# A product made three times over the same bank, in the scan of a four-layer hybrid network

## The chip, the core and the metric

The kernel runs on one core of a Trainium2 chip. The metric is the device time of one execution in microseconds (us). The core has five engines that run side by side, each with its own queue in program order: TensorE (PE; its weight loads are listed apart as PEld), VectorE (DVE), ScalarE (ACT), GpSimd (POOL) and SyncE (SP). ScalarE, SyncE and GpSimd also issue DMA transfers; in the profile a queue's own steps have a q behind the engine's name (ACTq). A pair of terms that come up often: a unit of the scan is one step of the list described below; a bank is a 128 x 512 float32 piece of PSUM, the memory that TensorE writes its products to.

## The reference

Four images of 96 channels and 64 x 64 pixels pass four layers: a selective scan in four directions, a deformable convolution, a Fourier mixing with a quantized feed-forward, and a linear attention with a second feed-forward. The change lies in the first layer's scan. Cut to it:

```python
delta = jax.nn.softplus(dts + delta_bias[None, :, :, None])
def step(h, inp):
    d_t, u_t, b_t, c_t = inp
    dA = jnp.exp(d_t[..., None] * A)
    h = dA * h + (d_t * u_t)[..., None] * b_t[:, :, None, :]
    y = jnp.einsum('bkdn,bkn->bkd', h, c_t)
    return (h, y)
```

There are 192 channels d, 16 states n per channel, 4 directions k, and 4096 pixels in sequence. Every channel's delta times u is spread over its 16 states and multiplied by b there.

## The kernel before

**The units.** `Layer0.scan` (line 773) runs over 1536 units: 4 images, 4 directions, 4 pieces of 1024 pixels, 3 groups of 64 channels, and in each group 8 units of 8 channels. A unit holds 8 channels x 16 states on the 128 partitions and 1024 pixels along the free dimension. Its steps, by method and line:

- `fetch` (823) issues, four units ahead, all on ScalarE's queue: `bc` (b and c of a piece, once in 24 units), `du` (line 845, two tiles at the first unit of each group, so once in 8 units), and `da` (line 858, delta spread over the states, each unit). `du` has delta u in three bf16 parts whose sum is the float32 value, 3 x 32 rows on 96 partitions, for 32 channels and 1024 pixels.
- `decay` (860, line 863) makes exp(A delta) on ScalarE, in place.
- `inflow` (865, line 869) spreads delta u over the states on TensorE. The stationary table `rep` has a 1 where row p, taken modulo 32, is the channel of the output partition. So one product of 96 rows both adds the three parts and copies each channel to its 16 states. Two products of 512 columns fill the two banks of `db`, of which there are two buffers.
- `recur` (878) multiplies `db` by b in place (line 882) and runs the recurrence along the pixels (line 885), both on VectorE.
- `weigh` (889, lines 892 and 894) keeps the last state and multiplies the states by c, on GpSimd.
- `total` (896, lines 907 and 912) sums over the states on TensorE, for two units at a time. `settle` and `store` copy the sum out and send it to DRAM.

**What sets the order.** In iteration n of the scan the program emits, in this order, the total of the units n-5 and n-4 (when n is odd), the product and the decay of unit n+1, the loads of unit n+4, the recurrence of n, and the weighing of n-2. A product of unit n+1 writes a buffer that the recurrence of unit n-1 has used, so it waits for that; the multiplication of unit n+1 comes after the recurrence of unit n on VectorE.

**The side work.** After every unit, steps of two other streams of work are put in: `ends` (the preparation of the next images, then layers 2 and 3) and `middle` (what follows the scan, and the deformable convolution). Which steps, and how many, is decided at build time by a planner, the class `Clock` (198). It keeps an estimated end of the work queued on each engine. Every step of the scan books its estimate with `clock.add`, every side step books what its `cost(...)` says. A side step may go in only if the estimated end of each engine that it needs is not further ahead of now than `AHEAD` (for TensorE 1.0 us), and now moves on by at least `PACE` = 4.7 us each unit:

```python
def has_room(self, work, ready):
    now = self.now()
    idle = self.idle if self.own is None else self.own
    if self.own is None and work[DVE] and self.beside >= BESIDE:
        return False
    first = next((e for e in (PE, ACT, DVE, POOL) if work[e]), None)
    if ready > (now if first is None else max(self.ends[first], idle)):
        return False
    return all(not w or e <= now + a for w, e, a in zip(work, self.ends, AHEAD))
```

The product of a unit books 0.9 us on TensorE (line 866), and its estimated end is also the earliest start that the planner gives the multiplication of that unit. What is left of the two streams when the units are done runs behind the scan. Steps of the side work on TensorE that are named later: the 3 x 3 convolution of layer 0 (line 653), the weighting of the sampled pixels (1237) and the Fourier matrices (1327).

## Time and profile before

| what | value |
|---|---|
| median of 3 runs | 9941.68 us (9924.21 to 9967.65) |
| the profiled execution | 9884.11 us, its span 9882.0 us |
| granted TensorE clock, mean | 0.761 |
| before the first product of a unit | 327 us |
| from the first product to the last | 8063 us |
| after it | 1492 us |
| the two products of a unit, busy time in all | 1191.5 us in 3072 instructions |
| a `du` load's issue on ScalarE's queue | 0.735 us median, 384 of them |

Times in the profile are from one execution. The busy time of an engine is the time in which it works on an instruction; a TensorE instruction's end is modelled, and a float32 product is recorded as two instructions. "PEclk" or "granted clock" is the share of full speed that TensorE's clock was granted. In a group of instructions the columns are line, engine, operation, output and inputs with their shapes and the count, then busy time in us and mean in ns of one, then the idle time of the engine ahead of it and what ended most of that. The chain is followed back from the last instruction to what released it, step by step.

### The profile page before, as it was taken

How to read it: one execution, taken by the hardware profiler on the slowest of the kernel's cores; microseconds unless marked ns; L12 is line 12 of the kernel's file. 1: busy time of each engine (PE TensorE's matmuls, PEld its weight loads, DVE VectorE, ACT ScalarE, POOL GpSimd, SP SyncE). 2: the span in 40 equal slices, each digit the busy share in tenths (PEclk: the TensorE clock that was granted, in tenths of full speed). 3: DMA queues.
4: the chain of work that ended last, by engine and by line, in shares of the span. 5: the costliest groups of instructions: out<-in, count | busy, mean ns of one | idle time of the engine just before them, and what ended most of it. 6: DMA issues, size and time to landing. Idle time of an engine off the chain costs nothing.

```text
span 9882.0 us, 101184 instructions
## 1 busy us (share of the span) xinstructions
PE 7523.3 (76%) x36536; PEld 3441.1 (35%) x36536; DVE 6913.6 (70%) x4545; ACT 4182.3 (42%) x5734; POOL 6722.5 (68%) x4947
## 2 busy tenths in 40 slices
PE   7565866686756679777678788777888777999797
PEld 2111311121123344211136553213565321687283
DVE  0488688877888887788888888788888887122111
ACT  3563655464544334555432334443323444211424
POOL 0695589657789997688899976567989556176101
PEclk9555856686767789766678898777898877899586
DMA  1566677666777877776787886667877756343010
GB/s 46 141 179 167 164 194 193 171 168 170 188 192 202 206 193 194 186 194 182 190 210 195 216 190 171 156 164 182 216 201 204 172 144 146 94 134 113 13 52 7
DMA packets 775689, 1606.32 MB, mean 163 GB/s; under 512 B 249333, under 2 KB 339561, under 8 KB 773078
## 3 DMA queue, kind: packets, MB, share of 16 engines
q10 hardware_dynamic: 300672, 985.79, 40.1%
q1 hardware_dynamic: 400790, 387.50, 14.6%
q0 software_dynamic: 73728, 226.57, 8.5%
q8 instruction: 290, 4.75, 0.2%
q14 instruction: 209, 1.71, 0.1%
HBM read 1343.23 MB, written 256.29 MB: 162 GB/s over the span
## 4 chain that ended last, share of the span: by engine, by line
PE 35%; POOL 19%; DVE 16%; DMA 15%; issue 8%; ACT 6%; ACTq 1%; SPq 1%; DVEq 0%; POOLq 0%
POOL hh L894 9%; PE ps L1237 8%; DVE hh L885 7%; DMA da<-de 5%; POOL g L1215 4%; PE pc L653 4%; DVE db L882 4%; PE f L1327 3%; DMA du<-du 3%; PE py L912 2%; PE po L1115 2%; PE db L869 2%; DMA g<-table,idx 1%; DVE g L1224 1%; POOL lw L742 1%
## 5 line engine op out<-in xcount | busy, mean ns | idle before, releaser
L894 POOL TENSOR_TENSOR hh<-hh,bc 128x1024 f32<-128x1024 f32 x1536 | 3652.2, 2379 | 331.5 <-DVE hh L885 215.3
L885 DVE TENSOR_TENSOR_SCAN hh<-da,st,db 128x1024 f32<-128x1024 f32 x1152 | 2703.7, 2347 | 345.3 <-ACT da L863 220.0
L882 DVE TENSOR_TENSOR db<-db,bc 128x1024 f32<-128x1024 f32 x1536 | 1868.8, 1217 | 586.6 <-PE db L869 584.0
L863 ACT ACTIVATE da<-da,w_al 128x1024 f32<-128x1024 f32 x1536 | 1740.1, 1146 | 913.0 <-DMA da<-de 530.7
L869 PE MATMUL db<-du,rep 96*128 96x512 bf16 x3072 | 1191.5, 481 | 1181.1 <-DVE hh L885 1072.0
L1215 POOL DMA_INDIRECT g<-table,idx x1152 | 1442.5, 1252 | 490.2 <-issue 223.5
L1237 PE MATMUL ps<-w_ident,g 128*96 128x128 f32 x9216 | 1236.6, 299 | 291.5 <-DVE g L1224 160.1
L912 PE MATMUL py<-hh,w_fold 128*32 128x512 f32 x6144 | 1223.6, 802 | 173.4 <-POOL hh L894 80.0
L1237 PEld LDWEIGHTS ps<-w_ident,g 128*96 128x96 f32 x9216 | 1185.9, 183 | 400.9 <-DVE g L1224 198.1
L869 PEld LDWEIGHTS <-rep 96*128 96x128 bf16 x3072 | 209.2, 103 | 2608.9 <-DVE hh L885 1783.5
L885 DVE TENSOR_TENSOR_SCAN hh<-da,db 128x1024 f32<-128x1024 f32 x384 | 878.1, 2287 | 89.7 <-ACT da L863 48.3
L1244 ACT COPY st<-ps 96x384 f32<-96x384 f32 x384 | 182.5, 476 | 1451.9 <-PE ps L1237 1349.8
L1224 DVE TENSOR_TENSOR g<-g,wt 128x3456 f32<-128x3456 f32 x128 | 526.0, 4109 | 334.2 <-DMA g<-table,idx 306.7
L892 POOL COPY st<-hh 128x1 f32<-128x1 f32 x1152 | 279.4, 243 | 696.1 <-DVE hh L885 667.9
L653 PE MATMUL pc<-pad,wc 96*128 96x512 f32 x1152 | 526.7, 607 | 27.1 <-DMA wc<-wc_d 24.8
L741 POOL TENSOR_TENSOR w<-w,ex 128x512 f32<-128x512 f32 x192 | 264.6, 1378 | 393.6 <-ACT w L738 383.1
L1473 POOL CAST xqf<-fl 96x512 fp8e5<-96x512 f32 x64 | 45.3, 716 | 652.6 <-DVE fl L1431 545.0
L912 PEld LDWEIGHTS py<-hh,w_fold 128*32 128x32 f32 x6144 | 178.7, 125 | 815.9 <-issue 430.0
L765 DVE TENSOR_TENSOR du<-ex,du 128x512 bf16<-128x512 f32 x192 | 275.2, 1433 | 189.7 <-ACT du L763 179.3
L731 PE MATMUL pd<-xd,dtw 7*64 7x512 f32 (+1 forms) x512 | 332.4, 955 | 49.9 <-DVE rl L744 39.9
L744 DVE SCALAR_TENSOR_TENSOR rl<-pd,lw 128x512 f32<-128x512 f32 x192 | 130.0, 677 | 291.3 <-POOL lw L742 288.7
L761 POOL TENSOR_TENSOR ex<-ex,du 128x512 f32<-128x512 f32 x192 | 233.0, 1213 | 136.2 <-ACT du L759 135.7
(239 smaller groups left out, 9345.4 us busy)
## 6 DMA issues: line engine op xcount, KB each, us to landing
da<-de ACTq DMA_DIRECT2D x1536, 512.0 KB
du<-du ACTq DMA_DIRECT2D x384, 192.0 KB
bc<-bcd ACTq DMA_DIRECT2D x128, 512.0 KB
du<-du SPq DMA_DIRECT2D x128, 384.0 KB
y<-yb SPq DMA_DIRECT2D x384, 128.0 KB
de<-rl SPq DMA_DIRECT2D x128, 256.0 KB
m<-in_dft SPq DMA_DIRECT2D x128, 256.0 KB
du<-du SPq DMA_DIRECT2D x128, 192.0 KB
```

The source lines that it names most:

```text
L653: nc.tensor.matmul(pp, lhsT=wc[:, q, g * 128 : (g + 1) * 128], rhs=pad[:, r0 + dy : r0 + dy + NR, dx : dx + W], start=(q == 0), stop=(q == 8),
L731: nc.tensor.matmul(o, lhsT=dtw[rows, q, m], rhs=xdbl[q, j][rows], start=True, stop=True)
L863: self.net.nc.scalar.activation(u.da, u.da, AF.Exp, scale=self.al[:, a : a + 1])
L869: self.net.nc.tensor.matmul(db[:, h, :], lhsT=self.rep[:96, u.s % 4, :], rhs=u.du[u.s // 4][:, h * CH : (h + 1) * CH], start=True, stop=True,)
L882: nc.vector.tensor_mul(u.db, u.db, u.bc[:, 0, :])
L885: nc.vector.tensor_tensor_scan(u.along(u.hh), u.along(u.da), u.along(u.db), first, ALU.mult, ALU.add)
L894: self.net.nc.gpsimd.tensor_mul(u.hh, u.hh, u.bc[:, 1, :])
L912: nc.tensor.matmul(py[p0 : p0 + 32], lhsT=self.fold[:, u.i, :], rhs=hc[:, h * CH : (h + 1) * CH], start=u.sums["add"] is None and u.i == 0 ...
L1215: nc.gpsimd.indirect_dma_start(out=g[:, k, :], out_offset=None, in_=self.tables[b % 2], in_offset=bass.IndirectOffsetOnAxis(ap=idx[:, 9 * ...
L1224: nc.vector.tensor_mul(g4, g4, w4.unsqueeze(2).to_broadcast([128, 36, C]))
L1237: nc.tensor.matmul(pt[:, k, :], lhsT=g[:, k0 + k, c * C : (c + 1) * C], rhs=net.ident, start=(c == 0), stop=(c == 3),)
L1327: nc.tensor.matmul(pt[64 * part : 64 * part + 64, c, :], lhsT=d[:, :, c0 + c], rhs=matrix[:, 64 * part : 64 * part + 64], start=True, stop ...
```

## The change

The products of a unit are made three times over, one set behind the other into the same two banks, each of them starting the bank anew, so that the last set stands. They have 128 rows instead of 96. The rows 96 to 127 of the table are set to zero, and the rows 96 to 127 of each `du` tile are filled by a second load of 32 rows of the first part, on the same queue, so that finite numbers meet the zeros. The planner's entry for the product goes from 0.9 to 1.8 us.

```diff
     rep = (p[:, None, None] % 32 == 8 * np.arange(4)[None, :, None] + p[None, None] % 8).astype(f)
+    rep[96:] = 0.0
...
-                t = sp.tile([96, T], BF16, name=f"du{u.key}_{q}", tag=f"du{q}")
-                nc.scalar.dma_start(t, self.du_d[b][k][:, c0 + 32 * q : c0 + 32 * q + 32, ts])
+                t = sp.tile([128, T], BF16, name=f"du{u.key}_{q}", tag=f"du{q}")
+                src = self.du_d[b][k][:, c0 + 32 * q : c0 + 32 * q + 32, ts]
+                nc.scalar.dma_start(t[:96], src)
+
+                nc.scalar.dma_start(t[96:], src[0])
...
-        u.spread = self.net.clock.add(PE, 0.9, self.scanned[1])
+        u.spread = self.net.clock.add(PE, 1.8, self.scanned[1])
         db = self.ps.tile([128, 2, CH], F32, name=f"db{u.key}", tag="db", bufs=2)
-        for h in range(2):
+
+        for h in 3 * (0, 1):
             self.net.nc.tensor.matmul(
                 db[:, h, :],
-                lhsT=self.rep[:96, u.s % 4, :],
+                lhsT=self.rep[:, u.s % 4, :],
```

## The prediction

> **What bounds the kernel now.** I read the busy shares first, then the stages, the chain of work that ended last, the groups and the waits around the db product, and last the timeline of TensorE.

> ```profile
> PE 7523.3 (76%) x36536; PEld 3441.1 (35%) x36536; DVE 6913.6 (70%) x4545; ACT 4182.3 (42%) x5734; POOL 6722.5 (68%) x4947
> ...
> PEclk9555856686767789766678898777898877899586
> ```

> No engine is full over the span, so the shares name no bound. What stands out is PEclk: TensorE is granted full speed only part of the time. The windows by stage (columns: stretch, length, busy time of PE, PEld, DVE, ACT and POOL with counts, granted clock, DMA share, GB/s), cut at the first and the last db product:

> ```profile
> 327.00:8390.00 8063.00, 6000.84 (x27253) 2459.51 (x27252) 6562.89 (x4169) 3618.22 (x4759) 6226.98 (x4535) 0.75 0.73 184
> 8390.00:9882.00 1492.00, 1294.92 (x8868) 903.77 (x8866) 319.70 (x325) 418.29 (x799) 458.54 (x377) 0.81 0.24 68
> ```

> The scan takes 8063 us for 1536 units, 5.25 us each; VectorE is busy 81% of it, GpSimd 77%, TensorE 74%, at a mean clock of 0.75. The 1492 us after it hold no product of the changed kind; TensorE alone is busy there. The chain:

> ```profile
> PE 35%; POOL 19%; DVE 16%; DMA 15%; issue 8%; ACT 6%; ACTq 1%; SPq 1%; DVEq 0%; POOLq 0%
> POOL hh L894 9%; PE ps L1237 8%; DVE hh L885 7%; DMA da<-de 5%; POOL g L1215 4%; PE pc L653 4%; DVE db L882 4%; PE f L1327 3%; DMA du<-du 3%; PE py L912 2%; PE po L1115 2%; PE db L869 2%; DMA g<-table,idx 1%; DVE g L1224 1%; POOL lw L742 1%
> ```

> The chain changes engines all the time, and the product itself (L869) is only 2% of it. Its group, its reader and the two waits between them:

> ```profile
> L885 DVE TENSOR_TENSOR_SCAN hh<-da,st,db 128x1024 f32<-128x1024 f32 x1152 | 2703.7, 2347 | 345.3 <-ACT da L863 220.0
> L882 DVE TENSOR_TENSOR db<-db,bc 128x1024 f32<-128x1024 f32 x1536 | 1868.8, 1217 | 586.6 <-PE db L869 584.0
> ```

> ```profile
> PE db L869 <- DVE hh L885: 1072.0, 492, 15.3
> PE db L869 <- DMA du<-du: 92.2, 25, 23.0
> DVE db L882 <- PE db L869: 584.0, 256, 21.4
> ```

> (Columns of the last: us in total, times, longest.) Both directions occur. In 492 units TensorE stands idle until a scan sets a db buffer free, 2.2 us each on average. In 256 units VectorE stands idle until the product is there, 2.3 us each. In between lie about 790 units in which neither shows an idle wait.

> [...] two stretches side by side, first windows, then TensorE's timeline (start, duration, ..., idle time before it):

> ```profile
> 2855.00:2866.00 11.00, 8.60 (x60) 4.71 (x58) 7.04 (x5) 8.91 (x12) 10.28 (x6) 1.00 0.63 162
> 2867.00:2894.00 27.00, 14.38 (x49) 5.65 (x50) 25.29 (x14) 6.23 (x6) 25.47 (x15) 0.50 0.91 222
> ```

> ```profile
> 2864.20 0.61 PE L869 MATMUL db<-du,rep 96*128 96x512 bf16 x2 [2.20 <-DVE hh L885]
> ...
> 2867.77 1.04 PE L869 MATMUL db<-du,rep 96*128 96x512 bf16 x2 [1.97 <-DVE hh L885]
> ```

> At clock 1.00 the pair takes 0.61 us, at 0.50 it takes 1.04 us. [...] 0.61 us less one isolated product (the shortest on record is 0.38 us) leaves 0.23; 1.04 less one at half clock (at most 0.63) leaves 0.41. [...] I take 128 rows instead of 96 at no time.

> **The change, part by part.**

> **Four more products per unit.** At full clock a unit's product goes from 0.61 to 0.61 + 4 x 0.216 = 1.47 us, at half clock from 1.04 to 1.04 + 4 x 0.427 = 2.75 us. Over 1536 units that is 1327 us of TensorE time at full clock. Most lies beside other work: from the moment a buffer comes free, VectorE is busy for a whole unit, 1.22 + 2.35 = 3.57 us, before it needs the result. A product that starts on time ends 2.1 us early instead of 2.96 at full clock, still 0.8 early at half. The 492 units with an idle TensorE (2.2 us) cover it too. Cover is gone where TensorE comes late. On the chain, L869 has 2% of 9882 = 198 us; that grows by the ratio 0.86/0.61 = 1.41 at full and 1.71/1.04 = 1.64 at half clock, so by 279 to 325: I take **+285**. Check from the waits: 256 late units x 0.86 = 220. Of the other 790 units some become late; I take 60 of them at 0.86, **+50**. Bounds of the two together: 0 (all of it moves into idle time) and 1536 x 0.86 = 1321.

> **The clock.** [...] Between 2867 and 2894 us TensorE is busy 14.4 of 27 us with six pairs; four more products each at half clock add 6 x 1.71 = 10 us, which makes 24.6 of 27[...]. I estimate the scan's mean clock at 0.90 after, instead of 0.75. TensorE has 35% of the chain, 3459 us, of which at most 1295 lie after the scan, so 2164 in it. If those scaled with the clock, a factor 0.75/0.90 would save a sixth, 360 us. But the lines that carry the chain on TensorE (L1237, L653) sit in stretches that already run fast:

> ```profile
> 1200.00:1600.00 400.00, 255.74 (x670) 43.55 (x670) 340.10 (x220) 233.35 (x322) 355.33 (x257) 0.58 0.75 192
> 3600.00:4000.00 400.00, 354.23 (x1772) 197.71 (x1765) 310.76 (x173) 180.38 (x198) 312.88 (x221) 0.92 0.75 191
> ```

> Where the clock is 0.58, VectorE (85%) and GpSimd (89%) are the full ones, and a faster TensorE buys little. I take half: **-180**. Bounds: 0, and 0.25 x 2164 = 541 at full clock throughout.

> **The second du load.** 384 more issues on ScalarE's queue at the median 0.735 us of the first (its line's view) are 282 us. They come in twos, every eighth unit; behind them on ScalarE stand the da loads (0.53 us each), the exponentials (1.15 us) and the copies of the side work. The loads are fetched four units ahead, some 20 us, which hides a delay of 1.5 us mostly. ScalarE and its queue have 7% of the chain: 7% of 282 is **+20**. The product now waits for two loads; the 25 waits for du get a second load issued 0.74 us later: 25 x 0.74 = **+18**. The bytes are 384 x 64 KB = 25 MB, 1.6% of 1606 MB; DMA has 15% of the chain, 1482 us, so **+22**. Together +60, bounds 0 and 282.

> **The planner.** The clock that decides how much side work goes between two units books 1.8 us for the product instead of 0.9. Of its pace of 4.7 us a unit it books 0.9 + 0.8 (half of the 1.6 for a pair's total), which leaves 3.0 us for side work on TensorE, and 2.1 after. Where side work on TensorE is thick (sampling and Fourier, some 2000 us or 380 units) I estimate that a tenth of the 3.0 no longer fits: 380 x 0.3 = 115 us goes later, at last behind the scan, where TensorE is 87% busy and nothing hides it. Units with less beside them give most of it back: **+40**, bounds -100 (lighter units run faster) and +230 (two tenths, nothing back).

> **The zeroed rows of the table** are written on the host and loaded once, as before: nothing.

> Sum: 285 + 50 - 180 + 60 + 40 = +255. The profiled execution took 9884.11 us (span 9882.0 and 2.1 around it), so 10139 after. The median of the three runs, 9941.68, is 0.58% above it; on that scale 10139 x 1.0058 = **10198 us**, +2.6%.

> **The rivals.**

> *The clock pays for everything (faster).* One mechanism: the added products hold the clock near 1.0 through the whole scan, and the half-clock stretches do lie on the chain in proportion. Then 541 us are saved, against 285 + 50 + 60 = 395 with no loss from the plan: -146, 9738, on the median's scale about 9795 us. For it: the chain is 35% TensorE and the clock stands at half for half of the scan's time. Against it: cold stretches are those with the least TensorE work on the chain. It decides from about three quarters of the 541 saved (395). Chance 0.22.

> *TensorE becomes the bound in thick stretches.* Between 3600 and 4000 us it is busy 354 of 400 us at 0.92, with 72 units; 72 x 0.86 = 62 us meet 46 idle ones. If all 2000 us of thick stretches behave so, 390 units pay 0.86 us more each, +335: 10474, or about 10535 us. For it: those waits are mostly queueing. Against it: the planner books the added time and thins the side work. Chance 0.17.

> *Hidden.* TensorE's idle waits (1072 us before this line alone) take it, clock and cost cancel, or the repeated products cost nothing since the plan has slack: about 9942 us, within 0.5%. That the change does not do what it says would look the same; nothing suggests it, as each repeated product starts its bank anew. Chance 0.14.

> **How the numbers follow.** The forecast has 0.47, its own range is 10030 to 10400. A change within 0.5%, about 50 us, cannot be told from none here: the three runs spread by 43 us. Faster 0.22; same 0.14; slower 0.47 + 0.17 = 0.64. For the range, half of the fast rival lies below 9830 and half of the thick one above 10600, so 9830 to 10600 leaves out 0.11 + 0.08.

> **What would show it.** Right: 9216 products at L869, sixes of about 1.5 us; scan clock about 0.90; the waits of VectorE for db at L882 above 584 us by 100 to 400; the product's share of the chain at 4 to 6%; the stage behind the scan longer by 0 to 150 us. Wrong on the clock: it stays below 0.8, or goes to 0.97 with VectorE's waits for db below 584. Wrong on the queues: ScalarE's waits for da rise by far more than 60 us, or the scan's end moves less than the tail does.

## The result, and the profile after

The changed kernel takes 10391.92 us (median of 4 runs, 10365.7 to 10405.35) against 9952.34 us before in the same comparison: a ratio of 1.0442, 95% interval 1.0408 to 1.0475. The forecast was 10198 us, +2.6%, range 9830 to 10600. The profiled execution took 10405.35 us, its span 10403.6.

Shares and clock, as they were shown of before:

```profile
PE 8353.2 (80%) x42680; PEld 3958.8 (38%) x42680; DVE 6935.3 (67%) x4545; ACT 4181.3 (40%) x5734; POOL 6684.7 (64%) x4947
...
PEclk9678987898889999888899999889998987987585
```

TensorE has 830 us more busy time, and the granted clock is clearly higher in the scan. Now the two stages, cut at the first and the last db product (before, then after; columns as in the prediction). The first product of before starts at 350.1 us and the last at 8385.4, not at 327 and 8390 as the table of before and the prediction have it, so the numbers of before differ a little from theirs:

```profile
350.00:8386.00 8036.00, 5996.96 (x27241) 2458.82 (x27241) 6554.81 (x4161) 3608.91 (x4743) 6209.96 (x4523) 0.75 0.73 184
8386.00:9882.00 1496.00, 1298.67 (x8878) 904.36 (x8876) 323.56 (x329) 418.29 (x799) 461.28 (x378) 0.81 0.24 68
```

```profile
349.00:8498.00 8149.00, 6522.57 (x32384) 2841.94 (x32385) 6518.50 (x4090) 3470.79 (x4479) 6133.17 (x4489) 0.89 0.73 184
8498.00:10404.00 1906.00, 1603.24 (x9881) 1039.16 (x9879) 381.55 (x400) 555.38 (x1063) 500.33 (x412) 0.76 0.20 57
```

This is the table to look at. The scan, in which all added work lies, grew by 113 us only. The stage behind it (the tail), in which nothing was added, grew by 410. It holds 1003 more products than before: side work that used to stand between the units now runs there. Read the two growths as approximate: the profiled execution of before (9884 us) is 68 us faster than the median beside which the changed kernel was timed, and that of after is 13 us slower than its own, so they add up to 523 us where the medians differ by 440. The page's chain and the groups around the product:

```profile
PE 38%; POOL 19%; DVE 16%; DMA 14%; issue 7%; ACT 6%; ACTq 1%; SPq 0%; DVEq 0%; POOLq 0%; another core or an unknown queue 0%
POOL hh L899 8%; PE db L874 7%; DVE hh L890 7%; POOL g L1220 5%; PE ps L1242 5%; PE pc L654 5%; DVE db L887 4%; PE f L1332 3%; DMA da<-de 3%; PE py L917 2%; DMA du<-du 2%; PE po L1120 2%; DMA g<-table,idx 1%; DVE g L1229 1%; POOL lw L743 1%
```

```profile
L874 PE MATMUL db<-du,rep 128*128 128x512 bf16 x9216 | 2503.8, 416 | 828.0 <-DVE hh L890 756.7
L890 DVE TENSOR_TENSOR_SCAN hh<-da,st,db 128x1024 f32<-128x1024 f32 x1152 | 2703.7, 2347 | 225.9 <-ACT da L867 90.6
L887 DVE TENSOR_TENSOR db<-db,bc 128x1024 f32<-128x1024 f32 x1536 | 1871.0, 1218 | 845.3 <-PE db L874 798.4
```

The lines have moved by five: L874, L887 and L890 are the former L869, L882 and L885. The product went from 2% to 7% of the chain (4 to 6% had been forecast), and VectorE waits 798 us for it instead of 584. TensorE's idle time ahead of it fell from 1072 to 757 us. Its timeline shows how long the sets of products take:

```profile
2862.37 2.74 PE L874 MATMUL db<-du,rep 128*128 128x512 bf16 x6 [2.07 <-DVE hh L890]
...
3716.55 2.76 PE L874 MATMUL db<-du,rep 128*128 128x512 bf16 x12
```

Six products at half clock (0.50 in that stretch) take 2.74 us (2.75 was worked out); at full clock (1.00) twelve, two units in a row, take 2.76. Before, a pair took 0.61 us at 1.00 and 1.04 us at 0.50, and two pairs in a row 1.04 us at 1.00:

```profile
3726.26 1.04 PE L869 MATMUL db<-du,rep 96*128 96x512 bf16 x4
```

So each further product costs 0.215 us at full clock ((1.04 less 0.61) / 2 before, (2.76 less 0.61) / 10 after) and 0.425 us at half ((2.74 less 1.04) / 4). These measured steps bear out the 0.216 and 0.427 in the prediction's sum, and with them its 0.86 and 1.71 us for four more.

### The profile page after: what moved, and what is told of

Same layout as the page of the kernel before. It is cut to its first block, busy times and chain, and to the rows that moved or that the text cites. A ratio compares the mean times of both kernels' runs of the same rounds, so it can differ in the third digit from the quotient of the medians.

```text
span 10403.6 us, 114007 instructions
## 1 busy us (share of the span) xinstructions
PE 8353.2 (80%) x42680; PEld 3958.8 (38%) x42680; DVE 6935.3 (67%) x4545; ACT 4181.3 (40%) x5734; POOL 6684.7 (64%) x4947
## 4 chain that ended last, share of the span: by engine, by line
PE 38%; POOL 19%; DVE 16%; DMA 14%; issue 7%; ACT 6%; ACTq 1%; SPq 0%; DVEq 0%; POOLq 0%; another core or an unknown queue 0%
POOL hh L899 8%; PE db L874 7%; DVE hh L890 7%; POOL g L1220 5%; PE ps L1242 5%; PE pc L654 5%; DVE db L887 4%; PE f L1332 3%; DMA da<-de 3%; PE py L917 2%; DMA du<-du 2%; PE po L1120 2%; DMA g<-table,idx 1%; DVE g L1229 1%; POOL lw L743 1%
## 5 line engine op out<-in xcount | busy, mean ns | idle before, releaser
L874 PE MATMUL db<-du,rep 128*128 128x512 bf16 x9216 | 2503.8, 416 | 828.0 <-DVE hh L890 756.7
L890 DVE TENSOR_TENSOR_SCAN hh<-da,st,db 128x1024 f32<-128x1024 f32 x1152 | 2703.7, 2347 | 225.9 <-ACT da L867 90.6
L887 DVE TENSOR_TENSOR db<-db,bc 128x1024 f32<-128x1024 f32 x1536 | 1871.0, 1218 | 845.3 <-PE db L874 798.4
L874 PEld LDWEIGHTS <-rep 128*128 128x128 bf16 x9216 | 856.7, 104 | 2858.4 <-DVE hh L890 1243.9
L1220 POOL DMA_INDIRECT g<-table,idx x1152 | 1394.2, 1210 | 412.7 <-issue 238.5
L1242 PE MATMUL ps<-w_ident,g 128*96 128x128 f32 x9216 | 1156.7, 286 | 194.7 <-DVE g L1229 119.4
L1242 PEld LDWEIGHTS ps<-w_ident,g 128*96 128x96 f32 x9216 | 1113.7, 173 | 318.7 <-DVE g L1229 142.9
L917 PE MATMUL py<-hh,w_fold 128*32 128x512 f32 x6144 | 1039.4, 689 | 172.5 <-ACT yb L928 81.3
L890 DVE TENSOR_TENSOR_SCAN hh<-da,db 128x1024 f32<-128x1024 f32 x384 | 878.1, 2287 | 80.2 <-ACT da L867 39.0
L742 POOL TENSOR_TENSOR w<-w,ex 128x512 f32<-128x512 f32 x192 | 266.1, 1386 | 371.3 <-ACT w L739 370.8
L1419 DVE TENSOR_TENSOR t<-t,o 96x512 f32<-96x512 f32 x64 | 80.4, 1261 | 405.0 <-PE o L1417 404.7
L654 PEld LDWEIGHTS pc<-pad,wc 96*128 96x128 f32 x1152 | 218.7, 193 | 311.1 <-issue 276.3
```

Of the source, the lines that this page charges most:

```text
L654: nc.tensor.matmul(pp, lhsT=wc[:, q, g * 128 : (g + 1) * 128], rhs=pad[:, r0 + dy : r0 + dy + NR, dx : dx + W], start=(q == 0), stop=(q == 8),
L874: self.net.nc.tensor.matmul(db[:, h, :], lhsT=self.rep[:, u.s % 4, :], rhs=u.du[u.s // 4][:, h * CH : (h + 1) * CH], start=True, stop=True,)
L887: nc.vector.tensor_mul(u.db, u.db, u.bc[:, 0, :])
L890: nc.vector.tensor_tensor_scan(u.along(u.hh), u.along(u.da), u.along(u.db), first, ALU.mult, ALU.add)
L917: nc.tensor.matmul(py[p0 : p0 + 32], lhsT=self.fold[:, u.i, :], rhs=hc[:, h * CH : (h + 1) * CH], start=u.sums["add"] is None and u.i == 0 ...
L1220: nc.gpsimd.indirect_dma_start(out=g[:, k, :], out_offset=None, in_=self.tables[b % 2], in_offset=bass.IndirectOffsetOnAxis(ap=idx[:, 9 * ...
```

## The experiments

All ratios are to the kernel before, run on the same chip in the same comparison; its medians lay at 9876 to 9897 us in those of the experiments. Scan is the stretch from the first to the last db product of each profiled execution, tail what follows it. These two are from one execution each, and that of e4 is 47 us slower than the median of its kernel; where a difference is small, the ratios decide.

| run | sets, rows, second load | entry, us | ratio (95%) | scan, us | its clock | tail, us |
|---|---|---|---|---|---|---|
| before | 1, 96, no | 0.9 | 1 | 8036 | 0.75 | 1496 |
| after | 3, 128, yes | 1.8 | 1.0442 (1.0408 to 1.0475) | 8149 | 0.89 | 1906 |
| e1_plan_old | 3, 128, yes | 0.9 | 1.0275 (1.0249 to 1.0301) | 8290 | 0.90 | 1494 |
| e2_plan_new | 1, 96, no | 1.8 | 1.0204 (1.0174 to 1.0233) | 7899 | 0.75 | 1840 |
| e3_rows | 1, 128, yes | 0.9 | 1.0065 (1.0045 to 1.0085) | 8074 | 0.78 | 1510 |
| e4_three_96 | 3, 96, no | 0.9 | 1.0272 (1.0249 to 1.0295) | 8320 | 0.84 | 1525 |
| e5_plan_045 | 1, 96, no | 0.45 | 0.9992 (0.9977 to 1.0007) | 8189 | 0.76 | 1319 |
| e6_five_sets | 5, 128, yes | 0.9 | 1.0763 (1.0738 to 1.0788) | 8736 | 0.95 | 1503 |
| e7_rows_no_load | 1, 128, no | 0.9 | 0.9962 (0.9945 to 0.9979) | 7986 | 0.78 | 1494 |
| e8_three_no_load | 3, 128, no | 0.9 | 1.0191 (1.0171 to 1.0211) | 8200 | 0.90 | 1487 |
| e11_fixed_96 | 1, 96, no (fixed tiles) | 0.9 | 0.9996 (0.9982 to 1.0010) | 8036 | 0.75 | 1489 |
| e10_rows_plan_06 | 1, 128, no | 0.6 | 0.9902 (0.9882 to 0.9922) | 8031 | 0.78 | 1389 |
| e12_load_on_sync | 1, 128, on SyncE's queue | 0.9 | 1.0013 (0.9999 to 1.0026) | 8054 | 0.77 | 1491 |
| e9_rows_dt | as e7, and more rows in the products of delta | 0.9 | 0.9951 (0.9935 to 0.9968) | 7970 | 0.79 | 1484 |

**Which part costs what.** The theory from the two stages above: the planner's entry moved side work behind the scan, and most of the loss is there. The rival: the products cost the time, and where the planner puts things only decides in which stage it shows. The first run changes one line of the changed kernel:

```diff
-        u.spread = self.net.clock.add(PE, 1.8, self.scanned[1])
+        u.spread = self.net.clock.add(PE, 0.9, self.scanned[1])
```

> The changed kernel with the planner's entry back at 0.9 us; the products stay at three sets of 128 rows. Theory A, the planner's entry pushed side work behind the scan: the stage behind the scan is back at about 1490 us (1901 in the changed kernel), the scan takes what the products really cost it, 50 to 250 us over the 8063 of before, and the whole is 1.005 to 1.025 of before. Rival B, the executed products cost the time whatever the planner books: the whole stays at 1.035 to 1.05, with the loss now inside the scan.

```profile
350.00:8640.00 8290.00, 6661.04 (x33385) 2928.14 (x33386) 6557.70 (x4162) 3609.62 (x4743) 6198.25 (x4523) 0.90 0.72 182
8640.00:10134.00 1494.00, 1292.18 (x8878) 901.54 (x8877) 321.29 (x328) 418.24 (x799) 462.70 (x377) 0.81 0.24 68
```

The tail is back to within 2 us, with the 8878 products of before. But the whole only fell to 1.0275, just above what the theory had said: the scan is 254 us longer than before, 141 more than in the changed kernel. VectorE's wait for the product is longer, too:

```profile
DVE db L887 <- PE db L874: 927.1, 420, 23.7
```

The second run changes the same line of the kernel before, from 0.9 to 1.8.

> The kernel before with the planner's entry at 1.8 us and nothing else. Theory A: the same order of side work as in the changed kernel, so the stage behind the scan is at about 1850 to 1900 us; the scan gets shorter than 8063 us by 0 to 150 us since less stands beside its units; the whole is 1.025 to 1.045 of before. Rival B: 0.995 to 1.01.

```profile
350.00:8249.00 7899.00, 5762.12 (x26234) 2388.50 (x26233) 6501.71 (x4089) 3469.54 (x4479) 6144.44 (x4489) 0.75 0.73 187
8249.00:10089.00 1840.00, 1547.47 (x9885) 1028.51 (x9884) 383.32 (x401) 556.56 (x1063) 497.18 (x412) 0.79 0.21 59
```

Not one instruction of the kernel is different, only the order, and it costs 2.0%: 1007 products go from the scan to the tail, the scan gets 137 us shorter, the tail 344 longer. TensorE's busy time in the tail rises by 249 us (1298.67 to 1547.47). The measured 2.0% lies between the answers of the two theories, so neither had it alone. The entry costs 2.0% by itself and 1.67% on top of the products (1.0442 less 1.0275). The rest is the products and the load.

**Products without rows and load, rows and load without products.** Both with the entry at 0.9, so in the order of before:

```diff
-        for h in range(2):
+        for h in 3 * (0, 1):
```

> The kernel before with three sets of products, of 96 rows, no second load, entry 0.9. Theory A: the products alone, scan 50 to 200 us longer, stage behind it about 1490 us, the whole 1.00 to 1.02. Rival B: 1.035 to 1.05. Against the first of these runs it shows what rows and second load do to the clock: [...].

It took 1.0272, the same as with 128 rows and the second load (1.0275). The clock tells why that is no proof that those cost nothing:

```profile
348.00:8668.00 8320.00, 7008.40 (x33384) 3015.32 (x33383) 6583.97 (x4163) 3611.67 (x4743) 6202.27 (x4524) 0.84 0.70 178
```

0.84 with 96 rows, 0.90 with 128. Rows and load in one set of products:

```diff
-        for h in 3 * (0, 1):
+        for h in range(2):
```

(against the first run)

> The kernel before with the second load of du, 128 rows and the zeroed rows of the table, one set of products, entry 0.9. Both theories: the order is that of before. If the second load costs what the prediction took (60 us) 1.006; if it is hidden, 0.997 to 1.003. The granted clock of the scan stays at 0.75 to 0.77 if only the number of products matters for it.

```profile
350.00:8424.00 8074.00, 5821.54 (x27240) 2436.08 (x27240) 6555.14 (x4161) 3608.39 (x4743) 6203.01 (x4523) 0.78 0.74 187
```

1.0065: the load is not hidden, though the clock rose to 0.78. To take the two apart, rows without the load:

```diff
+        self.blocks = 0
+        self.du_t = [[wp.tile([128, T], BF16, name=f"dut{m}{q}") for q in range(2)] for m in range(2)]
+        for t in self.du_t[0] + self.du_t[1]:
+            nc.gpsimd.memset(t[96:], 1.0)
...
-                t = sp.tile([128, T], BF16, name=f"du{u.key}_{q}", tag=f"du{q}")
+                t = self.du_t[self.blocks % 2][q]
...
-                nc.scalar.dma_start(t[96:], src[0])
```

> One set of products with 128 rows, entry 0.9, without the second load: four fixed du tiles take the place of the rotating ones, and their rows 96 to 127 are set to one once. If the 0.65% of the run with rows and second load was the second load: 0.995 to 1.001, with a scan clock of 0.77 to 0.78. If it was something of the rows themselves: 1.005 to 1.008.

0.9962, faster than before. The control, with the same tiles and 96 rows in the products:

> Control for the run with 128 rows and no load: the same four fixed du tiles, but only 96 rows in the products. If the rows made the gain: 0.998 to 1.002 of before, scan clock 0.74 to 0.755. If the fixed tiles made it: 0.995 to 0.997.

0.9996. So it is the rows that gain 0.34%, not the tiles. The scans of the two side by side, 96 rows first:

```profile
351.00:8387.00 8036.00, 6002.61 (x27240) 2473.30 (x27239) 6570.78 (x4162) 3609.82 (x4743) 6209.92 (x4523) 0.75 0.73 184
```

```profile
348.00:8334.00 7986.00, 5762.28 (x26830) 2431.66 (x27241) 6557.78 (x4162) 3607.64 (x4743) 6207.45 (x4523) 0.78 0.73 186
```

The same products in the same order, some 50 us less in these two executions (34 us by the ratios), the clock at 0.78 (some matmul records are missing in the second trace, so its busy time reads low). With three sets the same edit:

> The same with three sets of products, entry 0.9. If the second load costs about 0.65% here too, 1.018 to 1.024 (1.0275 with it); the scan clock near 0.90. If the load is hidden where TensorE is the late one: 1.025 to 1.03.

```profile
351.00:8551.00 8200.00, 6615.56 (x32861) 2913.34 (x33384) 6569.37 (x4162) 3609.03 (x4743) 6204.10 (x4523) 0.90 0.71 181
```

1.0191, so the second load costs 0.84% there (1.0275 less 1.0191), and 1.03% with one set (1.0065 less 0.9962): 80 to 100 us. Where in the load it lies was tried in the kernel of e3, with the issue on another queue:

```diff
-                nc.scalar.dma_start(t[96:], src[0])
+                nc.sync.dma_start(t[96:], src[0])
```

> The run with rows and second load (one set of products, entry 0.9; 1.0065 of before), with the second load issued on SyncE's queue instead of ScalarE's. Without the load that kernel ran at 0.9962. If the time that the issue takes from ScalarE's queue is what the load costs: 0.995 to 0.999. If it is the bytes or the second wait of the product: 1.003 to 1.008. SyncE's queue holds stores that wait for side work, so a load that gets stuck behind them would make it slower still, above 1.01, with more waiting for du on TensorE.

1.0013 (0.9999 to 1.0026), between the two answers. About half of the cost goes with ScalarE's queue, the other half stays; whether that is the bytes, the second wait or SyncE's queue is open.

Where the half on ScalarE's queue acts can be read from the program and the traces. In the iteration that fetches `du`, `settle` is emitted right behind the loads on ScalarE: it copies the finished sum `py` to `yb`. There is one buffer of `py`, so the next total on TensorE waits for that copy, and the products of the next unit stand behind the total. TensorE's wait for the copy with the second load (e3), then without it (e7):

```profile
PE py L912 <- ACT yb L928: 272.7, 80, 20.2
PE py L915 <- ACT yb L931: 131.9, 61, 9.9
```

With the load on SyncE's queue (e12) it is 172.9 us. How much of this wait turns into time of the kernel was not measured alone.

**What the clock pays.** More sets at a clock that can hardly rise further:

```diff
-        for h in 3 * (0, 1):
+        for h in 5 * (0, 1):
```

> The changed kernel with five sets of products instead of three, the planner's entry at 0.9. From one set to three (128 rows, same order) the scan grew by 216 us while its clock rose from 0.776 to 0.897. If the risen clock paid a part of that, two more sets, with little clock left to gain, cost clearly more: 350 to 700 us over three sets, 1.06 to 1.10 of before. If the clock pays nothing, two more sets cost the same as the first two, 216 us, give or take 80: 1.04 to 1.057.

```profile
349.00:9085.00 8736.00, 7628.85 (x38896) 3458.06 (x39528) 6569.28 (x4163) 3611.11 (x4743) 6204.57 (x4524) 0.95 0.68 173
```

```profile
DVE db L887 <- PE db L874: 1353.4, 522, 22.9
```

The second fence is the wait of VectorE for the product, 1353 us now. The ratio of 1.0763 is what was expected if the risen clock had paid a part. From one set to three (e3 to e1) the scan grew by 216 us while the clock went from 0.78 to 0.90. From three to five it grew by 446 us, for a rise of 0.05. The difference of 230 us is an upper estimate of what the clock paid for the first two sets: part of it can be queueing, since later sets meet a fuller TensorE. A second estimate takes pairs with the same number of products, by their ratios: 34 us (0.34%) for the rise from 0.75 to 0.78 in e7 against its control, 80 us (0.81%) for the rise from 0.84 to 0.90 in e8 against e4. Stretched to a rise of 0.12 that is 140 to 160 us. So the clock paid between 140 and 230 us; this is worked out and not measured alone.

**The planner's entry the other way, and a faster version.** The kernel before with 0.45:

> The kernel before with the planner's entry at 0.45 us instead of 0.9, nothing else. If the entry trades scan against tail evenly, the trend of 0.9 to 1.8 (scan 136 us shorter, stage behind it 343 longer) goes on the other way: scan 60 to 150 us longer, stage behind it 100 to 350 shorter, the whole 0.97 to 1.00. Rival: the order of before already has all side work in that can go in, since other limits than TensorE hold it back in the scan; then 0.995 to 1.01, with the stage behind the scan within 50 us of 1496.

0.9992: scan 153 us longer, tail 177 shorter. At 0.9 and 96 rows the two trade evenly. With 128 rows and 0.6:

> The run with 128 rows and no load, with the planner's entry at 0.6 us instead of 0.9. If scan and tail trade evenly between 0.45 and 0.9, as they did with 96 rows: 0.994 to 0.998, no different from that run. If the faster clock of 128 rows leaves room in the scan for more side work: 0.98 to 0.993.

```profile
349.00:8380.00 8031.00, 5805.72 (x27968) 2541.18 (x28405) 6532.15 (x4154) 3602.78 (x4759) 6156.38 (x4504) 0.78 0.72 184
8380.00:9769.00 1389.00, 1164.52 (x7705) 790.18 (x7710) 360.12 (x336) 417.71 (x783) 497.84 (x396) 0.84 0.27 75
```

0.9902, the fastest of all: the scan pays 45 us, the tail gives 105 (against e7). It is 1% faster than the kernel before. Whether 0.6 would do the same with 96 rows was not tried. A last try of rows, in the products of seven rows that make delta:

```diff
-            nc.tensor.matmul(o, lhsT=dtw[rows, q, m], rhs=xdbl[q, j][rows], start=True, stop=True)
+            nc.tensor.matmul(o, lhsT=dtw[:, h, q, m], rhs=xdbl[q, j], start=True, stop=True)
```

(`dtw` has a copy for each half, with zeros in the other rows.)

> On top of the run with 128 rows and no load, the products that make delta (7 rows of table and data, in the preparation of each image) get all 103 rows of the projected tile, against a table with zeros in the others; their number and their columns stay. If the clock follows the rows that a product uses, the windows of the preparation (400 to 800 and 1200 to 1600 us, clock 0.62 and 0.64 in that run) show 0.70 or more. If the rows of these few products do not matter to the clock, they stay within 0.03. In time, both: those windows are held by VectorE and GpSimd, so 0.985 to 0.998 of before.

0.9951 (0.9935 to 0.9968), no different from e7; the windows rose from 0.62 and 0.64 to 0.64 and 0.68, by less than 0.05 each. Undecided for the clock, nothing in time, as VectorE and GpSimd hold those windows (busy for 338 and 361 us of the 400 from 1200 on in e9, TensorE for 227).

## Why the prediction was right, and where its terms were off

It was right in the direction and in the mechanisms, and the measured 10392 us lies in the forecast's own range of 10030 to 10400, at its upper edge. The growth of 4.4% is well above the 2.6% of the sum: most costs came out somewhat larger, and one, the planner's, four times larger.

- **Four more products, +335, and the clock, -180: net +155.** Measured, with 128 rows and without load and entry, 1.91%, or 189 us (e8). The two halves were not measured alone. Stretched to the whole rise from 0.75 to 0.90, the rates of the two pairs above give 170 to 200 us for the clock, which leaves 360 to 390 for the products: by these estimates the clock's term was about right, the products' a little low. VectorE's wait for the product, forecast to rise by 100 to 400 us, rose by 214 in the changed kernel and 343 in e1 (927 us).
- **The clock after: 0.90 was forecast, 0.89 measured.** That they agree is in part luck. The 0.90 was the author's estimate from the number of products alone; no run had shown how far the clock would rise. Three sets of 96 rows reach only 0.84 (e4); I took 128 rows instead of 96 as nothing at all, an assumption for the time and for the clock. In time a product of 128 rows is indeed no slower than one of 96 (shortest 376 ns in both kernels). But the granted clock rose with the rows: 0.75 to 0.78 with one set (e11 to e7), 0.84 to 0.90 with three (e4 to e8), and the latter rise comes with 0.8% less time (1.0272 to 1.0191).
- **The second load, +60.** Measured 80 to 100 us. The queue was costed at 20 of the 60, by ScalarE's 7% of the chain; e12 puts about half of the measured cost, some 50 us, on it. The issues themselves are shorter than assumed (0.465 us in the median, not 0.735). What was missed is what stands behind them on ScalarE: the copy of the sum, for which the next total on TensorE waits. Fetching four units ahead does not move that copy away from the loads.
- **The planner, +40.** This is the term that failed by size: 1.67% on top of the products, 165 us (269 between the two profiled executions, which are from different comparisons), and 2.04% alone (e2). The prediction had the mechanism, side work pushed behind the scan, and mis-sized two of its steps. It took 115 us of TensorE time as moved; e2 moved 249, about the two tenths of its upper bound. And it let the lighter units "give most of it back": they gave 137 of 344 us (e2), two fifths. In the scan this work runs beside VectorE and GpSimd; in the tail little runs beside it (VectorE is busy 382 of 1906 us). The clock in the tail was lower, too: 0.81 before, 0.79 in e2, 0.76 after. Why the changed kernel's tail is 66 us longer than that of e2, with nearly the same products in it, is open. The sign that the prediction had named, a stage behind the scan longer by 0 to 150 us, showed it at once: 410.
- **The rivals.** That the clock pays for everything was wrong: it reached 0.89, not 1.0. That TensorE becomes the bound in thick stretches did not come. The prediction named against it that the planner would thin the side work there, but it does not come in e1 either, where the plan is not thinned: VectorE's waits for the product rise by 343 us, and the whole is still at 2.75%, not at that rival's 6%. Cut at the starts of the recurrence into 16 stretches of 96 units, e1 is longer than e3 by at most 32 us in one of them, 0.33 us a unit where the rival had 0.86, and TensorE is busy for 80% of e1's scan (6661 of 8290 us). The rival's number, 10535 us, is nearer to the measured 10392 than the forecast's 10198 is, but the cause it gives is not the one that the runs show.

Taken in the order e7, e3, e1, after, the steps are: rows -0.38%, load +1.03%, products with the clock's gain +2.10%, entry +1.67%. They add up to +4.42% by construction; in another order the shares differ (the entry 2.04% alone, the load 0.84% with three sets).

## What to carry to other kernels

Where a planner fills gaps by booked costs, a changed booking moves work even if no instruction changes; compare the stage in which nothing was edited first. Products added to keep TensorE busy can raise its clock and still lose: here the clock of the scan went from 0.78 to 0.90 (e3 to e1), and they got back, by the estimates, some 40 to 50% of what they cost. More rows in a product that is made anyway raised the clock here from 0.75 to 0.78, with 0.34% less time, once the extra rows came without a load. Before a load is called hidden, look at what stands behind its issue on the same queue.

## What the runs showed that was not expected

The busy share of TensorE does not rise with it. With one set, TensorE is busy for 75% of the scan of e11 (96 rows, 6003 of 8036 us) at a clock of 0.75, and for 72% of that of e3 (128 rows, 5822 of 8074 us) at 0.78. With three, it is busy for 84% in e4 (96 rows, 7008 of 8320 us) at 0.84, and for 80% in e1 (128 rows, 6661 of 8290 us) at 0.90. The kernel with the higher clock has the smaller busy share each time; a product takes longer at half clock, so part of that difference follows from the clock itself. How the clock is set was not shown, nor which property of the wider product counts, and the test on other products (e9) is undecided.
